# A graph-attention kernel's start-up: where the bound check's sums of squares, the last bias's rows and the residual additions stand

## The chip, the cores and the metric

The kernel runs on one core of a Trainium2 chip. The metric is device time in microseconds (us) of one execution, as a median of several runs. A core has five engines that work side by side, each through its own instructions in order: TensorE (PE in the profile, with PEld for its weight loads) multiplies matrices, VectorE (DVE) and ScalarE (ACT) do elementwise work and are the ones that read PE's results out of PSUM, GpSimd (POOL) does elementwise work in SBUF, and SyncE (SP) issues the DMA transfers. An instruction waits on semaphores until what it needs is there; everything behind it on the same engine waits with it.

## The reference

The input x is 64 graphs of 256 nodes with 512 features, in float32; all graphs share one adjacency matrix. Two layers follow, each on a layer norm with a ReLU, each added to x:

```python
h = jnp.maximum(_layernorm(x, axis=-1), 0.0)
x = x + _L0_gnn_ref(h, adj, L0_gnn_W, L0_gnn_a)
h = jnp.maximum(_layernorm(x, axis=-1), 0.0)
x = x + _L1_gnn_ref(h, adj, Wq, bq, Wk, bk, Wv, bv, Wo, bo)
```

The first is a graph attention: h W gives 256 features, their scores with two vectors are added pairwise, go through a leaky ReLU, a mask and a softmax, and weigh the same features; the result and h W stand side by side. The second is attention with 8 heads of 64 under the same mask, with the four weights Wq, Wk, Wv, Wo (512 x 512) and their biases.

## The kernel before

The 64 graphs are taken in 32 groups of two (GB = 2, NG = 32). Within a group, b is the graph and t one of its two tiles of 128 nodes. Everything stays in float32. Products with the weights are done in Strassen's manner with seven products instead of eight; for that the kernel adds and subtracts quarters of the weights once (`weight_sums`, `first_weight_sums`) and quarters of the operands in each group (`operand_sums`).

The softmax is done without subtracting the row's maximum. That is allowed only if the scores are bounded, so a bound check is computed from the weights: `judge` finds sums of squares of the weights and biases and some Gram matrices, and `conclude` turns these norms into a flag, `wrong`. If the flag is set, the whole work is done again by a general version (`any_inputs`); with the given inputs it is not.

Work is written as generators. Each `yield` ends a piece, and the main body calls `next` on them in an order written out by hand:

- `norms` is the first layer's norm over all groups (`first_norm`): mean and variance on VectorE (`measure`), the factor on GpSimd, xn on ScalarE, then a transposition of 32 x 32 blocks on VectorE into a tile xt, of which there is one buffer, written to DRAM (passed) and fetched back (moved) by DMA, and copied on ScalarE into hT0.
- `pieces` is the first layer for one group (`first_layer`): products ph, attention values e, products po, and the norm of the second layer through the same transposition into hT1.
- `products` is the second layer's projection of one group (`project`): for each of q, k and v seven products, in the order 1, 2, 6, 7, 5, 4, 3 of `seven`. Products 1, 6, 5 and 3 build up in one PSUM bank, 2, 4 and 7 in others. ScalarE copies intermediate sums out (kept_q, kept_k, kept_v; buffers with the tag "kept", three in turn), VectorE adds them to the later ones. PE may only go on with a bank when the copy or the addition that reads it is done.
- `verdict` is the bound check, and `bias` is `last_bias`: bv Wo + bo, added to the residual later. It makes the tile bv_rows on VectorE by four instructions from Wo and bv, sums it over the partitions by a matmul with a matrix of ones (pb), and adds bo to it (b_out).
- `residual(g)` adds b_out to x on GpSimd, two instructions for each graph.

In the start-up, group 0 goes through its first layer. Then the list `order` (line 1115) runs over the other 19 pieces of project(0); beside each stands which pieces of `norms` (n) and of `pieces` (s) follow. In this loop also stand the steps of the bound check (line 1127), of the last bias (line 1128), the weight sums of v and o and the residual addition for group 0 (line 1131).

Then comes the steady state: for each group g and each graph b in it, a string in `steps` (line 1135) orders the pieces. S computes the attention scores and exps of (g, b), m masks a pair of heads, u is a piece of project(g + 1), s one of first_layer(g + 2), n one of the norm of group g + 3, o one of the output products of the graph before (py, added into x by VectorE), f one of the row sums, r one of the residual and v a difference of values. weigh (products pr, then oT on VectorE) starts each graph.

`not_sooner` keeps an instruction behind the last one given to its engine in this way; other instructions may be moved a little by the scheduler of the framework. All matmuls keep the written order (`matmul`, line 136). Line 35 stands for all instructions of VectorE, ScalarE, GpSimd and most DMAs, and line 137 for all matmuls, since helpers record them; the names of tiles tell them apart.

Tiles with the same tag share buffers. In the version before, square_ones (the matrix of ones) lies in the buffer of o_sums, bv_rows in one of the three "kept" buffers, and squares, the output that nobody reads of the sums of squares, in the buffer of oT1.

Of the kernel before, what the change touches and what calls it, by code (L numbers as in the profile page):

```python
# [8 lines left out]
F32 = mybir.dt.float32  # L9
I32 = mybir.dt.int32  # L10
AF = mybir.ActivationFunctionType
ALU = mybir.AluOpType
AX = mybir.AxisListType

P = 128
# [8 lines left out]
LARGEST_VALUE = 1e4  # L24
# [33 lines left out]
def bounded(  # L58
# [27 lines left out]
    B, N, D = x.shape  # L86
    F1 = w0.shape[1]
    DH = 64
    HP = D // P
# [160 lines left out]
    gpsimd.memset(rexp, -0.5)  # L250
    ones = const.tile([P, S], F32, name="ones")
    gpsimd.memset(ones, 1.0)
    square_ones = big.tile([P, P], F32, tag="o_sums", name="square_ones", bufs=1)
    gpsimd.memset(square_ones, 1.0)

    def weight_sums(name, engine=vector):
# [16 lines left out]
    def last_bias():  # L273


        rows = att.tile([P, 2, D // 2], F32, tag="kept", name="bv_rows", bufs=3)
        for q in range(NQ):
            for half in range(2):
                of, by = w_sb["o"][:, half, 2 * q : 2 * q + 2, :], bv_col[:, half, q : q + 1]
                if q == half == 0:  # L280
                    not_sooner(vector, "tensor_scalar", rows, of, by, None, op0=ALU.mult)
                else:
                    vector.scalar_tensor_tensor(rows, of, by, rows, op0=ALU.mult, op1=ALU.add)
        yield
        pb = mm("pb")
        matmul(pb, square_ones, rows.rearrange("p o n -> p (o n)"), start=True, stop=True)
        yield
        not_sooner(vector, "tensor_add", b_out, pb, b_out)
        yield


    def judge():

        part = const.tile([P, 10], F32, name="part")
        vector.memset(part, 0.0)
        room = att.tile([P, 2 * HP + 1, P], F32, tag="p", name="room", bufs=1)
        heads = room[:, 2 * HP, :]  # L300
        vector.memset(heads, 0.0)
        for j in range(2):
            vector.memset(heads[j * DH : (j + 1) * DH, j * DH : (j + 1) * DH], 1.0)
        power = {}

        def bank(name):
            return mm(name).rearrange("p (h o) -> p h o", h=HP)

        for n, name in enumerate(("q", "k")):
            gram = bank(f"gram_{name}")  # L310
            for hp in range(HP):
                half, cols = hp // 2, slice(hp % 2 * P, (hp % 2 + 1) * P)
                for c in range(HP):
                    w = w_sb[name][:, c % 2, c // 2 * 2 + half, cols]
                    matmul(gram[:, hp, :], w, w, start=(c == 0), stop=(c == HP - 1))
            power[name] = room[:, n * HP : (n + 1) * HP, :]
            vector.tensor_mul(
                power[name], gram, heads[:, None, :].to_broadcast([P, HP, P])
            )
            yield  # L320
        for i in range(2):
            for n, name in enumerate(("q", "k")):
                square = bank(f"square_{name}{i}")
                for hp in range(HP):
                    a = power[name][:, hp, :]
                    matmul(square[:, hp, :], a, a, start=True, stop=True)
                if i < 1:
                    not_sooner(scalar, "copy", power[name], square)
                else:
                    scalar.activation(  # L330
                        power[name], square, AF.Square, accum_out=part[:, 8 + n : 9 + n]
                    )
                yield

        for _ in range(4):
            yield
        room = big.tile([P, D], F32, tag="oT1", name="squares", bufs=1)

        def squares(col, *srcs):
            sums = small.tile([P, HP], F32, tag="sums", name=f"sums{col}", bufs=2)  # L340
            for i, src in enumerate(srcs):
                to = room[:, : src.free_size()]
                if len(src.shape) == 3:
                    to = to.rearrange("p (a b) -> p a b", a=src.shape[1])
                not_sooner(
                    scalar, "activation", to, src, AF.Square, accum_out=sums[:, i : i + 1]
                )
            vector.reduce_sum(part[:, col : col + 1], sums[:, : len(srcs)], axis=AX.X)

        squares(2, *[w0_sb[:, c, 2:] for c in range(HP)])  # L350
        yield
        squares(3, *[w_sb["v"][:, :, i, :] for i in range(HP)])
        yield
        for i in range(2):
            squares(i, w0_sb[:, :, i])
        squares(4, bcol["q"])
        squares(5, bcol["k"])
        squares(6, bv_col)
        vector.reduce_max(part[:, 7:8], bad.rearrange("p a t -> p (a t)"), axis=AX.X)
        yield  # L360
        yield
        total = mm("total")[:, :10]
        matmul(total, square_ones, part, start=True, stop=True)
        norm = const.tile([P, 10], F32, name="norm")
        vector.tensor_scalar(norm, total, 1e-30, None, op0=ALU.add)
        power = const.tile([P, 10], F32, name="power")
        gpsimd.memset(power, 0.5)
        gpsimd.memset(power[:, 7:8], 1.0)
        gpsimd.memset(power[:, 8:10], 1.0 / 16)
        gpsimd.tensor_tensor(norm, norm, power, op=ALU.pow)  # L370
        norms_found.append(norm)
        yield
# [3 lines left out]
    def conclude():  # L376
        (norm,) = norms_found
        root = float(D) ** 0.5

        test = const.tile([P, 5], F32, name="test")  # L380
        side = const.tile([P, 2], F32, name="side")
        not_sooner(vector, "tensor_add", test[:, 0:1], norm[:, 0:1], norm[:, 1:2])
        vector.tensor_scalar(
            test[:, 0:1], test[:, 0:1], root / LARGEST_SCORE, None, op0=ALU.mult
        )
        not_sooner(vector, "tensor_scalar", side, norm[:, 8:10], root, None, op0=ALU.mult)
        vector.tensor_add(side, side, norm[:, 4:6])
        vector.tensor_mul(test[:, 1:2], side[:, 0:1], side[:, 1:2])
        vector.tensor_scalar(
            test[:, 1:2], test[:, 1:2], scale / LARGEST_SCORE, None, op0=ALU.mult  # L390
        )
        not_sooner(
            vector, "tensor_scalar",
            test[:, 2:3], norm[:, 2:3], root / LARGEST_VALUE, None, op0=ALU.mult
        )
        not_sooner(
            vector, "scalar_tensor_tensor",
            test[:, 3:4], norm[:, 3:4], root, norm[:, 6:7], op0=ALU.mult, op1=ALU.add
        )
        vector.tensor_scalar(  # L400
            test[:, 3:4], test[:, 3:4], 1.0 / LARGEST_VALUE, None, op0=ALU.mult
        )
        not_sooner(vector, "tensor_scalar", test[:, 4:5], norm[:, 7:8], 2.0, None, op0=ALU.mult)
        vector.tensor_scalar(test, test, 1.0, None, op0=ALU.is_le)
        held = const.tile([P, 1], F32, name="held")
        vector.tensor_reduce(held, test, axis=AX.X, op=ALU.min)
        vector.tensor_scalar(wrong, held[0:1, :], -1.0, 1.0, op0=ALU.mult, op1=ALU.add)
# [660 lines left out]
    def run(part):  # L1068
        for _ in part:
            pass  # L1070
# [40 lines left out]
    next(pieces)  # L1111
    next(verdict)
    next(verdict)
    next(norms)
    order = "n - s n sn - - ss ss s s - - - - s - s -".split()
    for i, parts in enumerate(order, 2):
        next(products)
        if i == 14:
            weight_sums("o", gpsimd)
        if i == 9:  # L1120
            first_weight_sums()
        if i in (2, 8):
            weight_sums("kv"[i // 7])
        for part in parts:
            if part != "-":
                next(norms if part == "n" else pieces, None)
        next(verdict, None)
        if i in (12, 14, 15):
            next(bias)
        if i == 17:  # L1130
            run(residual(0))
    run(verdict)


    steps = ("Smmnfuuuumonmnuofuusssosfsfssuvnofunonfosuo", "Ssmmfusmusmfuososfuosfrsuuonufrounfouunsous")
# [1 line left out]
    for g in range(NG):  # L1137
        products = project(g + 1) if g + 1 < NG else iter(())
        pieces = first_layer(g + 2) if g + 2 < NG else iter(())
        for b, parts in enumerate(steps):  # L1140
            if g == b == 0:

                parts = "Smmnfuuumnmnuufuussssfsfssuvnfunnfsuu"
            elif g == NG - 1:
                parts = "Smmoomoomooo"
            if waiting is not None:
                weigh(*waiting)
                late = outputs(*waiting[:2])
            i, count = -1, sum(part not in "frv" for part in parts)
            additions = residual(g + 1) if b == 1 and g + 1 < NG else iter(())  # L1150
            for part in parts:
                i += part not in "frv"
                if part == "u":
# [25 lines left out]
                if i == count // 2:  # L1179
                    if g == max(NG - 2, 0) and b == 1:  # L1180
                        conclude()
                    if g + 3 < NG:
                        load(g + 3, b)
        run(products)
        run(pieces)
    run(late)
# [372 lines left out]
```

## Time and profile before

| | us |
|---|---|
| median of 3 runs (2410.87 to 2412.3) | 2410.94 |
| the profiled execution, its own time | 2410.2 |
| its span, first to last instruction | 2408.5 |
| PE busy | 2380.4 (99%) |
| VectorE busy | 1687.9 (70%) |
| GpSimd busy | 1417.0 (59%) |
| ScalarE busy | 1022.0 (42%) |
| mean granted PE clock, as a share of full speed | 0.998 |
| PE busy from 0 to 20 / 20 to 40 / 40 to 60 us | 10.5 / 19.9 / 18.1 |
| PE busy from 60 to 80 / 80 to 100 / 100 to 120 us | 17.7 / 12.8 / 19.7 |
| PE clock from 60 to 80 / 80 to 100 us | 0.91 / 0.83 |

The span is one execution as the profiler recorded it; a little lies around it, so its own time is longer. Line by line, the timeline gives the start, the duration, the engine, the operation, the tile written and the tiles read, their shapes, and in brackets how long the engine was idle before and what ended that. A list of waits adds these idle times by pairs. Idle time of an engine that nobody waits for costs nothing.

### The profile page before, as it was taken

The page shows a single profiled execution, that of the slowest core. Times are in us where ns is not written, and L with a number is a line of the kernel's source. Part 1 is how long each engine was busy: PE and PEld are TensorE (multiplying, and loading weights), DVE is VectorE, ACT ScalarE, POOL GpSimd, SP SyncE. Part 2 cuts the span into 40 slices and gives each one's busy share as a digit, 9 for nine tenths or more (in the row PEclk, how much of TensorE's full clock was granted, in tenths as well). Part 3 has the DMA queues.
Part 4 walks back from the last instruction along what each step waited for, and adds up shares of the span by engine and source line. Part 5 has one row for each costly group of instructions (what it writes and reads, how often), then busy time and mean ns, then how long its engine had stood idle before and what let it go on. Part 6 is the DMA issues. An engine that isn't in the chain of part 4 may idle for free.

```text
span 2408.5 us, 42960 instructions
## 1 busy us (share of the span) xinstructions
PE 2380.4 (99%) x15772; PEld 2005.6 (83%) x15772; DVE 1687.9 (70%) x3338; ACT 1022.0 (42%) x2017; POOL 1417.0 (59%) x1282
## 2 busy tenths in 40 slices
PE   8899999999999999999999999999999999999998
PEld 7688888888888888888888888888888888888886
DVE  7576766777667767667777677776677676676665
ACT  5444443444444444434444444444344444343431
POOL 3566657555566556565556665565655565655652
PEclk9999999999999999999999999999999999999999
DMA  6244455544454444555444544444454445444331
GB/s 210 75 141 139 138 158 148 154 151 136 140 161 150 145 145 136 154 151 160 149 138 138 157 148 154 141 143 143 153 167 145 136 136 159 150 148 152 110 106 46
DMA packets 272041, 343.76 MB, mean 143 GB/s; under 512 B 25424, under 2 KB 217168, under 8 KB 271824
## 3 DMA queue, kind: packets, MB, share of 16 engines
q1 hardware_dynamic: 271824, 340.95, 45.8%
q8 instruction: 126, 2.06, 0.4%
q14 instruction: 91, 0.75, 0.1%
HBM read 177.22 MB, written 163.64 MB: 142 GB/s over the span
## 4 chain that ended last, share of the span: by engine, by line
PE 96%; DVE 1%; DMA 1%; ACT 1%; issue 0%; POOL 0%; SPq 0%; DVEq 0%; ACTq 0%; POOLq 0%
PE pv L137 16%; PE py L137 16%; PE pq L137 16%; PE pk L137 16%; PE sc L137 10%; PE pr L137 9%; PE ph L137 8%; PE po L137 4%; DMA w_sb<-in_L_gnn_W_dram 0%; DVE st L35 0%; DVE bv_rows L35 0%; DVE x L35 0%; ACT xn L35 0%; PE total L137 0%; DMA own<-line 0%
## 5 line engine op out<-in xcount | busy, mean ns | idle before, releaser
L35 POOL TENSOR_TENSOR p<-p 128x512 f32<-128x512 f32 x248 | 380.7, 1547 | 492.2 <-DVE p L35 478.7
L35 ACT ACTIVATE xn<-x,factor 128x512 f32<-128x512 f32 x256 | 194.4, 806 | 322.3 <-POOL factor L35 322.2
L35 DVE TENSOR_TENSOR p<-p,maskT 128x1024 f32<-128x1024 f32 x254 | 325.8, 1302 | 3.7 <-ACT p L35 3.7
L35 DVE TENSOR_TENSOR x<-py,x 128x256 f32<-128x256 f32 x448 | 186.0, 416 | 192.0 <-PE py L137 185.8
L35 ACT ACTIVATE p<-sc 128x512 f32<-128x512 f32 x512 | 257.6, 625 | 145.0 <-PE sc L137 128.3
L35 POOL TENSOR_TENSOR parts<-parts 128x512 f32<-128x512 f32 x248 | 248.5, 1002 | 82.6 <-DMA parts<-rows 59.0
L137 PE MATMUL py<-wo_sb,oT 128*128 128x256 f32 x1024 | 262.4, 379 | 0.6 <-DVE oT L35 0.6
L137 PE MATMUL sc<-q,k 64*128 64x256 f32 x2048 | 252.4, 390 | 0.6 <-DVE oT L35 0.6
L137 PEld LDWEIGHTS sc<-q,k 64*128 64x128 f32 x2048 | 204.5, 186 | 49.0 <-issue 25.9
L137 PE MATMUL pk<-hT,wk_sb 128*128 128x256 f32 x1024 | 244.7, 382 | 0.0
L137 PE MATMUL pq<-hT,wq_sb 128*128 128x256 f32 x1024 | 240.0, 382 | 0.3 <-ACT kept_q L35 0.3
L137 PE MATMUL pv<-wv_sb,hT 128*128 128x256 f32 x1024 | 238.4, 381 | 1.0 <-DVE k L35 1.0
L137 PE MATMUL pr<-p,v 128*32 128x256 f32 x4096 | 234.2, 380 | 0.0
L137 PEld LDWEIGHTS pq<-hT,wq_sb 128*128 128x128 f32 x1024 | 191.8, 190 | 35.8 <-issue 9.9
L35 POOL TENSOR_TENSOR factor<-factor,rexp 128x2 f32<-128x2 f32 x128 | 120.8, 943 | 169.0 <-DVE factor L35 168.8
L137 PEld LDWEIGHTS pv<-wv_sb,hT 128*128 128x128 f32 x1024 | 195.6, 191 | 29.2 <-DVE k L35 1.4
L137 PEld LDWEIGHTS py<-wo_sb,oT 128*128 128x128 f32 x1024 | 194.2, 190 | 28.2 <-DVE oT L35 1.1
L137 PEld LDWEIGHTS pk<-hT,wk_sb 128*128 128x128 f32 x1024 | 189.7, 190 | 33.3 <-issue 9.9
L137 PEld LDWEIGHTS pr<-p,v 128*32 128x32 f32 x4096 | 126.8, 110 | 97.8 <-issue 15.6
L137 PE MATMUL py<-wo_sb,o_sums 128*128 128x256 f32 x768 | 197.6, 380 | 0.5 <-DVE x L35 0.5
L137 PE MATMUL pk<-sums,wk_sb 128*128 128x256 f32 x768 | 182.8, 381 | 2.3 <-ACT kept_k L35 2.3
L137 PE MATMUL pq<-sums,wq_sb 128*128 128x256 f32 x768 | 181.5, 379 | 1.9 <-ACT kept_q L35 1.9
(148 smaller groups left out, 4055.7 us busy)
## 6 DMA issues: line engine op xcount, KB each, us to landing
passed<-xt SPq DMA_DIRECT2D x124, 512.0 KB, 3.1
moved<-passed SPq DMA_DIRECT2D x496, 128.0 KB, 3.4
rows<-p SPq DMA_DIRECT2D x124, 512.0 KB, 3.4
parts<-rows SPq DMA_DIRECT2D x496, 128.0 KB, 3.0
x<-in_x_dram SPq DMA_DIRECT2D x64, 512.0 KB, 4.4
out_dram<-x SPq DMA_DIRECT2D x62, 512.0 KB, 4.0
own<-line SPq DMA_DIRECT2D x31, 256.0 KB, 3.1
wq_sb<-in_L_gnn_Wq_dram SPq DMA_DIRECT2D x2, 512.0 KB, 9.2
```

Of the source, the lines that this page charges most:

```text
L35: instruction = getattr(self.engine, operation)(*args, **kwargs)
L137: in_order(nc.tensor.matmul(*args, **kwargs))
```

## The change

Five edits belong together.

1. The sums of squares leave the start-up. The loop over `order` no longer steps the bound check; instead each group from g = 2 on steps it once, in its second graph (at the ninth counted piece), until it is through: the first layer's weight in group 2, Wv in group 3, the score columns in group 4, the biases in group 5, the matmul `total` and the roots in group 6. The squares' unread output takes a "kept" buffer each time, since oT1 is in use by then. By that time the weights hold the sums and differences for the seven products, so the norms of two of them are multiplied by the square root of 3 (`changed`), a looser bound. The first layer's weight is taken with its two score columns (258 instead of 256 numbers).
2. square_ones gets a buffer of its own.
3. bv_rows lies in the buffer of oT0. Its first piece stands where it stood, after piece 12 of project(0); the matmul pb comes after piece 18 instead of 14 and the addition to b_out after piece 19 instead of 15.
4. In `order`, pieces of the norm of group 2 move: they came at pieces 1 (ahead of the list), 2, 5 and 6 and now come at 3, 5, 13 and 15. The weight sums of v move from piece 8 to 7, those of the first layer from 9 to 5, those of o from 14 to 13.
5. The residual additions of all groups form one sequence, of which each r takes the next piece. Those of group 0 leave the start-up: the string of the first graph gets an r, and the last graph of all gets one too. In each group, the two places take (g, 1) and (g + 1, 0) instead of (g + 1, 0) and (g + 1, 1).

```diff
@@ -250,7 +250,7 @@
     gpsimd.memset(rexp, -0.5)
     ones = const.tile([P, S], F32, name="ones")
     gpsimd.memset(ones, 1.0)
-    square_ones = big.tile([P, P], F32, tag="o_sums", name="square_ones", bufs=1)
+    square_ones = const.tile([P, P], F32, name="square_ones")
     gpsimd.memset(square_ones, 1.0)
 
     def weight_sums(name, engine=vector):
@@ -273,7 +273,7 @@
     def last_bias():
 
 
-        rows = att.tile([P, 2, D // 2], F32, tag="kept", name="bv_rows", bufs=3)
+        rows = big.tile([P, 2, D // 2], F32, tag="oT0", name="bv_rows", bufs=1)
         for q in range(NQ):
             for half in range(2):
                 of, by = w_sb["o"][:, half, 2 * q : 2 * q + 2, :], bv_col[:, half, q : q + 1]
@@ -332,12 +332,9 @@
                     )
                 yield
 
-        for _ in range(4):
-            yield
-        room = big.tile([P, D], F32, tag="oT1", name="squares", bufs=1)
-
         def squares(col, *srcs):
             sums = small.tile([P, HP], F32, tag="sums", name=f"sums{col}", bufs=2)
+            room = att.tile([P, D], F32, tag="kept", name=f"squares{col}", bufs=3)
             for i, src in enumerate(srcs):
                 to = room[:, : src.free_size()]
                 if len(src.shape) == 3:
@@ -347,17 +344,17 @@
                 )
             vector.reduce_sum(part[:, col : col + 1], sums[:, : len(srcs)], axis=AX.X)
 
-        squares(2, *[w0_sb[:, c, 2:] for c in range(HP)])
+        squares(2, *[w0_sb[:, c, :] for c in range(HP)])
         yield
         squares(3, *[w_sb["v"][:, :, i, :] for i in range(HP)])
         yield
         for i in range(2):
             squares(i, w0_sb[:, :, i])
+        yield
         squares(4, bcol["q"])
         squares(5, bcol["k"])
         squares(6, bv_col)
         vector.reduce_max(part[:, 7:8], bad.rearrange("p a t -> p (a t)"), axis=AX.X)
-        yield
         yield
         total = mm("total")[:, :10]
         matmul(total, square_ones, part, start=True, stop=True)
@@ -376,6 +373,9 @@
     def conclude():
         (norm,) = norms_found
         root = float(D) ** 0.5
+
+
+        changed = 3.0**0.5
 
         test = const.tile([P, 5], F32, name="test")
         side = const.tile([P, 2], F32, name="side")
@@ -391,11 +391,11 @@
         )
         not_sooner(
             vector, "tensor_scalar",
-            test[:, 2:3], norm[:, 2:3], root / LARGEST_VALUE, None, op0=ALU.mult
+            test[:, 2:3], norm[:, 2:3], changed * root / LARGEST_VALUE, None, op0=ALU.mult
         )
         not_sooner(
             vector, "scalar_tensor_tensor",
-            test[:, 3:4], norm[:, 3:4], root, norm[:, 6:7], op0=ALU.mult, op1=ALU.add
+            test[:, 3:4], norm[:, 3:4], changed * root, norm[:, 6:7], op0=ALU.mult, op1=ALU.add
         )
         vector.tensor_scalar(
             test[:, 3:4], test[:, 3:4], 1.0 / LARGEST_VALUE, None, op0=ALU.mult
@@ -1111,25 +1111,21 @@
     next(pieces)
     next(verdict)
     next(verdict)
-    next(norms)
-    order = "n - s n sn - - ss ss s s - - - - s - s -".split()
+    order = "- n s n s - - ss ss s s n - n - s - s -".split()
     for i, parts in enumerate(order, 2):
         next(products)
-        if i == 14:
+        if i == 13:
             weight_sums("o", gpsimd)
-        if i == 9:
+        if i == 5:
             first_weight_sums()
-        if i in (2, 8):
+        if i in (2, 7):
             weight_sums("kv"[i // 7])
         for part in parts:
             if part != "-":
                 next(norms if part == "n" else pieces, None)
-        next(verdict, None)
-        if i in (12, 14, 15):
+        if i in (12, 18, 19):
             next(bias)
-        if i == 17:
-            run(residual(0))
-    run(verdict)
+    additions = (piece for g in range(NG) for piece in residual(g))
 
 
     steps = ("Smmnfuuuumonmnuofuusssosfsfssuvnofunonfosuo", "Ssmmfusmusmfuososfuosfrsuuonufrounfouunsous")
@@ -1140,14 +1136,13 @@
         for b, parts in enumerate(steps):
             if g == b == 0:
 
-                parts = "Smmnfuuumnmnuufuussssfsfssuvnfunnfsuu"
+                parts = "Smmnfuuumnmnuufuussssfsfssuvnfrunnfsuu"
             elif g == NG - 1:
-                parts = "Smmoomoomooo"
+                parts = ("Smmoomoomooo", "Smrmoomoomooo")[b]
             if waiting is not None:
                 weigh(*waiting)
                 late = outputs(*waiting[:2])
             i, count = -1, sum(part not in "frv" for part in parts)
-            additions = residual(g + 1) if b == 1 and g + 1 < NG else iter(())
             for part in parts:
                 i += part not in "frv"
                 if part == "u":
@@ -1181,6 +1176,8 @@
                         conclude()
                     if g + 3 < NG:
                         load(g + 3, b)
+                if b == 1 and i == 8 and g >= 2:
+                    next(verdict, None)
         run(products)
         run(pieces)
     run(late)
```

## The prediction

> **What bounds the kernel now.** I read the page first. TensorE is busy for nearly the whole span:
>
> ```profile
> PE 2380.4 (99%) x15772; PEld 2005.6 (83%) x15772; DVE 1687.9 (70%) x3338; ACT 1022.0 (42%) x2017; POOL 1417.0 (59%) x1282
> ```
>
> So only 28.1 us of idle TensorE (2408.5 - 2380.4), and time at a reduced clock, can be won. The list of TensorE's waits says where they are (us in total, times, longest):
>
> ```profile
> PE pb L137 <- DVE bv_rows L35: 6.2, 1, 6.2
> PE pk L137 <- ACT kept_k L35: 2.3, 1, 2.3
> PE pq L137 <- ACT kept_q L35: 2.2, 2, 1.9
> ...
> PE pv L137 <- DVE k L35: 1.0, 1, 1.0
> ```
>
> Each happens once, in the start-up. From 140 to 2370 us the table by stretches shows PE busy for all of every stretch I asked for (200.00 of 200.00 from 200 to 400). TensorE's timeline places the waits (start, us, in brackets idle before):
>
> ```profile
> 65.73 3.16 PE L137 MATMUL pk<-sums,wk_sb 128*128 128x256 f32 x8 [2.34 <-ACT kept_k L35]
> 68.69 2.46 PE L137 MATMUL po<-H,e 128*128 128x257 f32 x8
> ...
> 81.00 1.99 PE L137 MATMUL pv<-wv_sb,hT 128*128 128x256 f32 x8 [0.99 <-DVE k L35]
> 89.19 2.08 PE L137 MATMUL pb<-bv_rows,square_ones 128*128 128x512 f32 x2 [6.19 <-DVE bv_rows L35]
> 91.05 3.21 PE L137 MATMUL pv<-wv_sb,hT 128*128 128x256 f32 x8
> ```
>
> Eight matmuls of 256 columns normally start 1.73 us apart. After the two long waits they take 2.96 (65.73 to 68.69) and 3.05: the granted clock is 0.60 and 0.55 from 66 to 70, and 0.50 to 0.57 from 88 to 94. Each long wait is paid for again. The timeline of all engines shows who is late:
>
> ```profile
> 62.84 0.41 ACT L35 ACTIVATE squares<-w_sb 128x256 f32<-128x256 f32 x1
> ...
> 64.86 0.82 ACT L35 ACTIVATE kept_k<-pk,bk_sb 128x256 f32<-128x256 f32 x2
> ...
> 83.12 1.30 DVE L35 STREAM_TRANSPOSE xt<-xn 128x512 f32<-128x512 f32 x2 [2.17 <-DMA passed<-xt]
> 84.34 0.45 DVE L35 TENSOR_SCALAR bv_rows<-wo_sb,bv_col 128x512 f32<-128x512 f32 x1
> 84.83 4.31 DVE L35 SCALAR_TENSOR_TENSOR bv_rows<-wo_sb,bv_col,bv_rows 128x512 f32<-128x512 f32 x3
> ```
>
> kept_k stands behind four squares on ScalarE; bv_rows stands on VectorE behind a transpose that waits for its only xt buffer to be written out.
>
> **The Trainium skill.** "TensorE: Matmul & The Clock Gate", Part 1 (the HAM clock gate): the clock halves after an idle window of about 3.4 us and is restored after about as long of work, in free-running windows. The trace agrees: about 4 us near half clock after 2.34 and after 6.19 us, none after 1.89. "SBUF — State Buffer", Who interferes with whom: VectorE with two SBUF inputs and GpSimd exclude each other. The trace agrees: o_sums takes 0.42 us alone, 1.38 to 1.49 beside GpSimd (320.3 to 324.4). "DMA: Bandwidth & Descriptors", the SWDGE path's anatomy, gives about 2.0 us fixed; these transfers go by SP, so I use the trace: xt freed 2.6 us after issue.
>
> **The change on the path.** From pq at 50.72 to the first sc at 102.82 are 52.1 us. Work in it: 18 products at 1.73, two po pairs at 1.73, pb 0.86 (512 columns), total 0.14, and 0.33 of issue: 35.9. The other 16.2 are waits (1.89 + 2.34 + 0.99 + 6.19 = 11.4), reduced clock (5.25 for pk and po against 3.45, 4.91 for pb and pv against 2.58: 4.1) and restarts (0.7). I replay this stretch in the new order with the old durations.
>
> kept_q: xn of group 2 (GpSimd's factor is there at 52.2) now stands behind both kept_q, not ahead. They run at 50.9 and 52.6; pq goes on at 52.44 instead of 54.49, saving 2.05. The next two pq follow without a wait, and pk starts at 57.6.
>
> kept_k: xn of group 2's second half and 4 squares leave ScalarE. It does e (own still lands at 56.3), exp to 60.2, q to 60.95, kept_k to 61.7; pk waits 0.7 from 61.05 instead of 2.34. That is shorter than the 1.89 that cost no clock, so 1.8 comes back too. pk runs at 61.75 instead of 65.73, its end 5.2 earlier; total's 0.14 leaves; last pk ends at 73.85.
>
> pv and bv_rows: factor at 72.1, xt transposes to 73.4, k to 74.05; pv at 74.1 (wait 0.25), 6.9 early. The next transposes still wait for xt (73.4 + 2.6 = 76.05), end 77.4; bv_rows follows: 0.45, a v addition, then 0.75 + 1.86 + 1.64 beside GpSimd's wo_sb, done at 82.85. But pb now stands behind five pv products, ending at 82.7: wait 0.15 for 6.19, no clock loss (2.3). After pb and two pv, sc starts at 87.6: **15.2 us earlier**. Bounds for this step: 16.3 if nothing remains, 11 if half the replayed margins fail and the clock dips once.
>
> **What the moves may cost.** The second xt of group 2 is moved past two kept_v, two v additions and, on SP, past passed and moved of group 1 (1 + 4 + 1 + 4 issues, 1.74 us per four). Replayed: transposes end at 87.7, passed lands at 90.4; moved waits as before for its buffer (ScalarE's hT copies), lands near 97. Those hT copies also slip behind four exps, ending at 91.7 (4.1 us after sc starts, before 1.7), so GpSimd's sums begin 2.3 us later against TensorE; its pair additions then overlap less with VectorE, and about 0.5 of the lag is left where ph needs group 2's sums. Before, they were 0.4 to 0.7 ahead. Cost 0.3, between -0.3 and 1.5 (oT to sc then had 0.56 of wait already).
>
> b_out leaves the way of sc's banks: added at 88.4, the fifth bank is needed at 89.5. Four residual additions (4.95 us) leave GpSimd at 95.7; two go into its 10.1 us idle at 133, two into the later slots. In each group the two slots keep their number of additions and take x one half later: ready at 305.7, needed by output additions some 20 us later. Without that cover, up to 2.5 us a group.
>
> Squares in the steady steps stand on ScalarE after the third kept_k:
>
> ```profile
> 289.18 0.84 ACT L35 ACTIVATE kept_k<-pk,bk_sb 128x256 f32<-128x256 f32 x2 [0.69 <-PE pk L137]
> 297.85 1.52 ACT L35 ACTIVATE xn<-x,factor 128x512 f32<-128x512 f32 x2 [7.82 <-POOL factor L35]
> ```
>
> Four of w0 take 4 x 0.54 = 2.2 us, four of wv 4 x 0.75 = 3.0, the small ones 0.33 each; all fit in 7.82. Without cover: 2.2 + 3.0 + 0.7 + 1.0 = 6.9. What waits behind them on ScalarE is that xn, then k and pv's copies; VectorE waits for them in eight reductions of 0.16 that stand after po's second reciprocal (293.3), when the squares are over (293.0 at the latest). Their buffer, one of three of the kept kind, was last read by the k addition of the same project, long done. In group 6, total is 0.14 on TensorE, and GpSimd's power (1.96 us) now stands ahead of a pair sum and of factor; behind them are xn, moved and the row sums, with 0.5 to 2 us of slack. I take 0.2 in all (0 to 1). square_ones' own buffer and three multiplications by a constant cost nothing: no instruction more.
>
> The end: the last half's two residual additions now follow GpSimd's mask there, in the last stretch:
>
> ```profile
> 2367.40 2.43 POOL L35 TENSOR_TENSOR p<-p,maskT 128x1024 f32<-128x1024 f32 x1 [9.80 <-ACT p L35]
> ...
> 2370.32 1.22 DVE L35 TENSOR_TENSOR p<-p,maskT 128x1024 f32<-128x1024 f32 x1
> ```
>
> They run from 2369.8 to 2372.4 beside two such VectorE masks, which take 1.7 to 2.25 beside GpSimd elsewhere (181.25, 111.57). py's additions wait behind the masks, and TensorE behind these (0.26 and 0.20 idle already). Cost 1.2, between 0 and 2.
>
> Sum: 15.2 - 0.3 - 0.2 - 1.2 = **13.5 us**. The profiled execution took 2410.2 (span 2408.5 and 1.7 around it): 2396.7. It lies 0.7 below the median 2410.94, so **2397.4**.
>
> **Rivals.**
> (A) As summed: 2395.5 to 2399.5, chance 0.62.
> (B) Part of the start-up wait comes back: bv_rows later than the five pv products, or group 1's sums later. For it: margins of 0.15 and 0.5 us. Against: all precede with the same durations. A 2.3 us wait with its 1.8 of clock, or both ends of the costs above: gain 7 to 11, 2399.5 to 2404; 0.23.
> (C) The spread squares are not hidden, and stall TensorE in five groups: 13.5 - 6.9, about 2404 to 2408. The 7.82 us speaks against: 0.07.
> (D) Slower: the residual additions, now half a group later, make py's additions wait in about 30 groups. Decides from 13.5 / 30 = 0.45 us a group; with 1 us, 2427. Against: 20 us of margin; and from the ninth group on nothing but the half of x in these additions differs in the order of any engine: 0.04.
> (E) It does not do what it says: the check with the looser sqrt(3) bound fails and the whole work is done again, above 4000 us. A W of 512 x 256 at variance 1/512 has norm 16; 16 x 1.73 x 22.6 / 10000 = 0.06, far from 1: under 0.01. Better than A (no contention at the end): 0.03.
>
> **The numbers.** Time: A's 2397.4. The range takes A, what is better, and B: 2393 to 2404.5. A difference of 0.2%, 4.8 us, is about what a measurement of this kernel can tell. Faster: better and A and B but for a little, and some of C: 0.90; same: rest of B and C: 0.06; slower: D, E: 0.04.
>
> **What would show it.** TensorE's waits: pb under 1 us, pk by kept_k near 0.7, none of 1.9 by kept_q; clock 1.00 from 60 to 100; first sc of group 0 near 87.6; PE still full from 140 to 2365; masks near the end above 1.5 us. Wrong would be: a new wait of ph or pq on GpSimd's sums near 95 to 110, of pb on bv_rows above 2 us, or idle TensorE in groups 2 to 6.

## The result, and the profile after

The changed kernel takes 2400.05 us (median of 5 runs, 2398.31 to 2401.28); the kernel before, in runs beside it, 2410.94 (2410.36 to 2413.55). The ratio is 0.9952, with a 95% interval of 0.9937 to 0.9967: 11 us or 0.5% faster, 2.6 us less than the 13.5 predicted. Run a second time, beside the first experiments, it took 2398.18 (2397.80 to 2398.51) against 2411.88, 13.7 us faster. One kernel thus moves by 2 to 3 us from one session to the next.

The page's line of TensorE (PE) keeps its 99% in a shorter span:

```profile
PE 2378.2 (99%) x15772; PEld 2005.0 (84%) x15772; DVE 1693.1 (71%) x3338; ACT 1021.4 (43%) x2017; POOL 1418.4 (59%) x1282
```

TensorE's list of waits (us in total, times, longest) has lost pb's wait of 6.2 and the kept_q wait of 1.9; in their place stands one for oT, and a small one for GpSimd's sums:

```profile
PE sc L137 <- DVE oT L35: 2.0, 1, 2.0
PE ph L137 <- DVE prod L35: 1.9, 1, 1.9
PE py L137 <- DVE x L35: 1.3, 3, 0.9
...
PE ph L137 <- POOL sums_xn L35: 0.5, 1, 0.5
PE pk L137 <- ACT kept_k L35: 0.5, 1, 0.5
```

TensorE's timeline of the changed kernel shows the start-up without a gap from pv to the first scores, pb taking its 0.86 us between two products, and then the two new waits:

```profile
63.05 1.99 PE L137 MATMUL pk<-sums,wk_sb 128*128 128x256 f32 x8 [0.52 <-ACT kept_k L35]
...
75.27 3.72 PE L137 MATMUL pv<-wv_sb,hT 128*128 128x256 f32 x16
...
84.00 1.02 PE L137 MATMUL pb<-bv_rows,square_ones 128*128 128x512 f32 x2
...
88.41 3.92 PE L137 MATMUL sc<-q,k 64*128 64x256 f32 x32
...
107.55 1.16 PE L137 MATMUL ph<-w_more,sums_xn 128*128 128x129 f32 x8 [0.55 <-POOL sums_xn L35]
...
126.63 4.40 PE L137 MATMUL sc<-q,k 64*128 64x256 f32 x22 [2.00 <-DVE oT L35]
```

ScalarE makes kept_k right after q, and VectorE has bv_rows ready at 82.9 (79.70 + 3.21), 1.1 us before TensorE asks for it:

```profile
61.44 0.82 ACT L35 ACTIVATE q<-pq,bq_sb 128x256 f32<-128x256 f32 x2
62.15 0.84 ACT L35 ACTIVATE kept_k<-pk,bk_sb 128x256 f32<-128x256 f32 x2
...
78.60 0.45 DVE L35 TENSOR_SCALAR bv_rows<-wo_sb,bv_col 128x512 f32<-128x512 f32 x1
79.09 0.69 DVE L35 TENSOR_TENSOR v<-pv,kept_v 128x512 f32<-128x512 f32 x1
79.70 3.21 DVE L35 SCALAR_TENSOR_TENSOR bv_rows<-wo_sb,bv_col,bv_rows 128x512 f32<-128x512 f32 x3
```

The squares now stand on ScalarE in the steady steps (here group 2), and the xn behind them still waits for its factor:

```profile
278.01 0.84 ACT L35 ACTIVATE kept_k<-pk,bk_sb 128x256 f32<-128x256 f32 x2 [0.69 <-PE pk L137]
278.74 0.42 ACT L35 ACTIVATE squares<-w_sb 128x258 f32<-128x258 f32 x1
...
280.68 0.19 ACT L35 ACTIVATION_READ_ACCUMULATOR squares<-w_sb 128x1 f32 x1
287.35 1.52 ACT L35 ACTIVATE xn<-x,factor 128x512 f32<-128x512 f32 x2 [6.48 <-POOL factor L35]
```

In the last group, the residual on GpSimd runs beside two of VectorE's masks, and py waits behind them:

```profile
2359.30 3.48 POOL L35 TENSOR_TENSOR x<-x,b_out 128x512 f32<-128x512 f32 x2
2359.83 1.82 DVE L35 TENSOR_TENSOR p<-p,maskT 128x1024 f32<-128x1024 f32 x1
...
2362.04 1.13 PE L137 MATMUL py<-wo_sb,o_sums 128*128 128x256 f32 x4 [0.86 <-DVE x L35]
2362.24 1.62 DVE L35 TENSOR_TENSOR p<-p,maskT 128x1024 f32<-128x1024 f32 x1
```

Cutting the span at marks that every kernel has shows where the time went. The marks are TensorE's first product pq on sums, its first pv, its first sc, the pk product after the second score stage, and the pr products of the last graph; each number is a difference of two starts in the timelines.

| stretch, us | before | after | after again |
|---|---|---|---|
| start to pq | 48.99 | 50.27 | 50.44 |
| pq to pv | 32.01 | 25.00 | 24.58 |
| pv to sc | 21.82 | 13.14 | 13.14 |
| sc to pk | 39.32 | 42.55 | 40.16 |
| pk to the last pr | 2250.44 | 2252.16 | 2252.12 |
| last pr to end | 15.92 | 16.38 | 16.16 |
| span | 2408.5 | 2399.5 | 2396.6 |

The start-up gave 15.7 and 16.1 us between pq and sc. Of it, 3.2 in the first trace but only 0.8 in the second went back between sc and pk, 1.7 between pk and the last pr, and 0.2 to 0.5 after it; 1.3 to 1.5 were lost before the first pq.

### The profile page after: what moved, and what is told of

Its sections match the earlier page's. It is cut to its first block, busy times and chain, and to the rows that moved or that the text cites. A ratio compares the mean times of both kernels' runs of the same rounds, so it can differ in the third digit from the quotient of the medians.

```text
span 2399.5 us, 42951 instructions
## 1 busy us (share of the span) xinstructions
PE 2378.2 (99%) x15772; PEld 2005.0 (84%) x15772; DVE 1693.1 (71%) x3338; ACT 1021.4 (43%) x2017; POOL 1418.4 (59%) x1282
## 4 chain that ended last, share of the span: by engine, by line
PE 96%; DMA 1%; DVE 1%; ACT 1%; POOL 0%; issue 0%; SPq 0%; ACTq 0%; DVEq 0%; POOLq 0%
PE pv L137 16%; PE pk L137 16%; PE py L137 16%; PE pq L137 16%; PE sc L137 10%; PE pr L137 9%; PE ph L137 8%; PE po L137 4%; DMA x<-in_x_dram 0%; SPq L35 0%; DMA w_sb<-in_L_gnn_W_dram 0%; ACT e L35 0%; DMA line<-rows 0%; POOL x L35 0%; POOL parts L35 0%
## 5 line engine op out<-in xcount | busy, mean ns | idle before, releaser
L35 POOL TENSOR_TENSOR factor<-factor,rexp 128x2 f32<-128x2 f32 x128 | 115.6, 903 | 179.9 <-DVE factor L35 179.7
```

Of the source, the lines that this page charges most:

```text
L35: instruction = getattr(self.engine, operation)(*args, **kwargs)
```

## The experiments

The first four runs are of one session, on one chip, beside the kernel before at 2411.88 us; the last four are of a later one, on another chip, beside the kernel before at 2410.76. Where a run of the second session is compared with the repeat, which is of the first, a difference of 2 to 3 us in the time alone proves little, and the stretches of the traces decide.

**The changed kernel again.** No edit. It is there to tell what the change does from what varies by itself.

> The changed kernel a second time, unaltered, as the measure of what varies from one profiled execution to the next. Two things of its first trace are not explained by any instruction that the change moves: TensorE was already 1.28 us late at the first product of the projection (pq at 50.27 us, before 48.99), and the DMA that brings own for group 2 took 4.7 us from issue to landing (before 3.7), which made TensorE wait 2.00 us for oT ahead of the second score stage and cost 1.1 us of clock. If both vary by chance, this trace shows pq near 49 and own landing in 3 to 3.8 us, the wait for oT near 1.0 (0.56 of before and some 0.5 for the later sums of group 1), and a span near 2397. Rival: the residual additions, which now run on GpSimd just then (120.17 to 122.69), delay own or the e behind it; then the wait of 2.0 us and the 1.1 us of clock come back here, whatever the start does.

Measured: 2398.18 us against 2411.88 beside it, ratio 0.9942 (0.9929 to 0.9956). The late start stayed (50.44), the wait for oT fell to 0.71 us with no loss of clock. The two traces' lists of DMA issues in the window around it (KB each, us from issue to landing) show why, first that of the first trace, then that of the repeat:

```profile
own<-line SPq DMA_DIRECT2D x1, 256.0 KB, 4.7
```

```profile
own<-line SPq DMA_DIRECT2D x1, 256.0 KB, 3.4
```

The residual stands at the same place in both, so the rival falls: what made 2.00 us of 0.71 is own's landing. In the first trace e's wait was put down to the residual (3.00 <-POOL x); but own landed 0.1 us before e there, and in the repeat e starts while the residual is still running:

```profile
119.94 2.54 POOL L35 TENSOR_TENSOR x<-x,b_out 128x512 f32<-128x512 f32 x2
121.20 1.71 ACT L35 ACTIVATE e<-own,H 128x256 f32<-128x256 f32 x4 [1.71 <-DMA own<-line]
```

So e doesn't wait for the residual, and the label named the wrong partner of a wait that has several. All five traces with the changed order on ScalarE (below) bear it out: own landed after 4.7, 4.2, 3.7, 3.4 and 3.0 us, and sc waited 2.00, 1.52, 1.03, 0.71 and 0.66. Why own's landing varies was not tested.

The start to pq is not explained by any edit; it lies between 48.25 and 50.44 in the traces. Of the 1.28 us between the first two traces, 0.63 is the landing of the first weight (VectorE's prod began at 10.43 us before, 11.06 after), and the rest is the first group of 16 products ph, which took 5.69 us before, 6.34 after and 6.79 in the repeat. What sets these is open.

**Bias and residual alone.** Edits 2, 3 and 5 on the kernel before:

```diff
-        if i in (12, 14, 15):
+        if i in (12, 18, 19):
             next(bias)
-        if i == 17:
-            run(residual(0))
     run(verdict)
+    additions = (piece for g in range(NG) for piece in residual(g))
```

with the two buffers and the strings as in the change.

> The kernel before with edits 2, 3 and 5 only: last bias's rows in the buffer of oT0 and pb four pieces later, and the residual additions in one sequence; the squares and the norm pieces stay where they were. From the timeline of before: pv starts at 81.0 as before, four more products follow without a wait, bv_rows is ready at 89.1 and pb comes at 89.65. My theory, that each edit's own wait goes and the gains add: pb's wait of 6.19 falls below 0.5, its 2.3 us of reduced clock goes, the first sc comes 8.5 to 8.8 us earlier against pq; the end costs 1.1 and the group-0 residual 0 to 1, so 2403.5 (7 us faster). Rival, that the norm pieces and squares carry the gain: pb still waits several us for bv_rows and this kernel is within 2 us of before.

Measured: 2404.68 us (2403.52 to 2405.66), ratio 0.9970 (0.9957 to 0.9982), 7.2 us faster; pb waits for nothing. TensorE's timeline:

```profile
66.84 2.00 PE L137 MATMUL pk<-sums,wk_sb 128*128 128x256 f32 x8 [2.34 <-ACT kept_k L35]
68.68 1.90 PE L137 MATMUL po<-H,e 128*128 128x257 f32 x8
...
79.09 1.99 PE L137 MATMUL pk<-sums,wk_sb 128*128 128x256 f32 x8 [1.37 <-DVE k L35]
82.12 3.72 PE L137 MATMUL pv<-wv_sb,hT 128*128 128x256 f32 x16 [1.04 <-DVE k L35]
...
90.93 1.13 PE L137 MATMUL pb<-bv_rows,square_ones 128*128 128x512 f32 x2
```

From pq to pv it takes 32.01 us, as before to the hundredth; from pv to sc 13.32 instead of 21.82. Two things follow. The bias edit is worth 8.5 us, all of it after pv. (No run has edit 3 without edit 5, but between pv and sc TensorE waited for nothing but bv_rows before, so the residual had no part in it.) And the reduced clock after pk's wait was worth nothing by itself here: the same wait of 2.34 us cost no clock this time (1.84 us from pk to po instead of 2.96), but the time came back as a wait of 1.37 for k on VectorE. VectorE's chain, with the reductions of the squares in it, was later than TensorE. These are its first reciprocals of po, before and here:

```profile
70.81 0.16 DVE L35 RECIPROCAL ri<-po 128x1 f32<-128x1 f32 x1
71.92 0.16 DVE L35 RECIPROCAL ri<-po 128x1 f32<-128x1 f32 x1
```

Counted from pq, they start at 21.82 and 21.81 us, though po itself came 1.1 us sooner here (18.57 for 19.70).

Two waits of the changed kernel are in this kernel too, with the norm pieces in the old order. So they don't come from edit 4:

```profile
114.59 1.16 PE L137 MATMUL ph<-w_more,sums_xn 128*128 128x129 f32 x8 [0.55 <-POOL sums_xn L35]
...
132.32 3.29 PE L137 MATMUL sc<-q,k 64*128 64x256 f32 x22 [0.66 <-DVE oT L35]
```

**Squares alone.** Edits 1 and 2 on the kernel before (the squares take the form of the change, `order` and the rest that of before):

```diff
-        next(verdict, None)
         if i in (12, 14, 15):
             next(bias)
@@
+                if b == 1 and i == 8 and g >= 2:
+                    next(verdict, None)
```

> The kernel before with edits 1 and 2 only: squares spread over the steady steps. My theory: four squares (2.0 us with their reads) leave the way of kept_k, pk waits 0.3 instead of 2.34 us and its 1.2 to 1.8 us of reduced clock goes; all that follows is 3.8 us earlier, since the chain through po, the factor, the two transposes and bv_rows is paced by it, and pb still waits 6.2 us. Steady steps cost 0.6. In all 3.2 us faster, 2407.7. Rival 1: pb's wait absorbs it, since bv_rows is ready no sooner: within 1 us of before. Rival 2: the squares are not hidden in groups 2 to 6, up to 6.9 us are lost again: slower than before by 3.

Measured: 2405.05 us (2404.81 to 2406.55), ratio 0.9974 (0.9964 to 0.9984), 6.8 us faster, twice what I expected. pq to pv takes 27.40 us (4.6 less): pk's wait 2.02, clock 1.79, total 0.14, and some 0.7 of waiting for k ahead of pv, which I had not counted. pv to sc takes 1.4 less, 1.07 of it in pb's wait, since bv_rows' three instructions took 3.21 us here and 4.31 before. In both, GpSimd's additions for wo_sb run beside them. Which of the two engines is held up differs, first before, then here:

```profile
85.61 1.85 DVE L35 SCALAR_TENSOR_TENSOR bv_rows<-wo_sb,bv_col,bv_rows 128x512 f32<-128x512 f32 x1
85.66 1.26 POOL L35 TENSOR_TENSOR wo_sb<-wo_sb 128x512 f32<-128x512 f32 x1 [5.51 <-DVE bv_rows L35]
...
81.45 0.75 DVE L35 SCALAR_TENSOR_TENSOR bv_rows<-wo_sb,bv_col,bv_rows 128x512 f32<-128x512 f32 x1
81.56 1.76 POOL L35 TENSOR_TENSOR wo_sb<-wo_sb 128x512 f32<-128x512 f32 x1 [4.19 <-DVE bv_rows L35]
```

pb still waits, and still costs clock:

```profile
83.93 2.08 PE L137 MATMUL pb<-bv_rows,square_ones 128*128 128x512 f32 x2 [5.12 <-DVE bv_rows L35]
85.80 2.87 PE L137 MATMUL pv<-wv_sb,hT 128*128 128x256 f32 x8
88.50 1.89 PE L137 MATMUL pv<-wv_sb,sums 128*128 128x256 f32 x8
```

The stretch from pk to the last pr is 0.54 us longer than before. Neither rival holds.

**Squares and norm pieces.** Edits 1, 2 and 4, with the bias at pieces 12, 14 and 15, its buffer and the residual as before (the diff is against the changed kernel, and leaves out the buffer and the strings):

```diff
-        if i in (12, 18, 19):
+        if i in (12, 14, 15):
             next(bias)
-    additions = (piece for g in range(NG) for piece in residual(g))
+        if i == 17:
+            run(residual(0))
```

> The kernel before with edits 1, 2 and 4: squares spread and the norm pieces and weight sums reordered, the last bias and the residual as before. My theory: kept_q's 1.9 us and kept_k's 2.34 us and its clock go, pv starts 6.9 us earlier; bv_rows stands behind the second transposition, which waits for its xt buffer as before, so pb still waits 6 to 6.5 us and costs 2.3 us of clock: the first sc comes 7 us earlier against pq. With 0.5 to 1 for group 1's later sums and the steady squares this is 6 us faster, 2405. With the 7 of the bias and residual alone it would make up the whole gain of 11 to 13.5, so the edits add. Rival, that pb's wait takes over what is saved ahead of it: less than 2 us faster, the wait for bv_rows then near 11 us.

Measured: 2403.25 us (2401.89 to 2404.93), ratio 0.9964 (0.9951 to 0.9978), 8.6 us faster (6 expected). pq to pv takes 24.58 us, exactly as in the repeat of the changed kernel, 7.4 less than before; pv to sc 21.74, as before, with pb waiting 5.43 and then 3.0 us of clock lost:

```profile
80.52 2.08 PE L137 MATMUL pb<-bv_rows,square_ones 128*128 128x512 f32 x2 [5.43 <-DVE bv_rows L35]
```

So the gain splits cleanly: edits 1 and 4 make pq to pv, edit 3 makes pv to sc, and from pq to sc the two sum up (7.5 + 8.5 = 16.0, with all edits 16.1). The ScalarE order of before is kept here, and ph and sc wait for nothing, with edit 4 in.

**Without the norm pieces.** The changed kernel with `order`, the weight sums' places and the first norm piece of before:

```diff
+    next(norms)
-    order = "- n s n s - - ss ss s s n - n - s - s -".split()
+    order = "n - s n sn - - ss ss s s - - - - s - s -".split()
```

> The changed kernel without edit 4: squares spread, last bias and residual moved, but the norm pieces and weight sums in the order of before. The runs so far gave, from the first product on sums (pq) to the first score product, 8.5 us for the bias and residual alone, 6.0 for the squares alone and 7.5 for squares with norms. If the edits add, the first score product comes 14.5 us earlier here (39.3 us after pq, before 53.83), with the wait of 1.9 us for kept_q back, and the kernel is about 1.5 us slower than the changed one: 2399.7. Rival, that pb's wait hid the norm pieces' gain and without it edit 4 is worth more: kept_q's 1.9 and a wait of pv or sc for k come back, 3 us or more slower than the changed kernel, 2401.5.

Measured: 2400.71 us (2399.25 to 2402.11), ratio 0.9959 (0.9946 to 0.9973), 2.5 us slower than the repeat. pq to sc takes 40.53 us, not 39.3: edit 4 is worth 2.8 us here and 1.5 without edit 3. My theory, that the edits add, missed this; the rival's 3 us is nearer, and for its reason: without edit 3, pb's wait and its clock swallowed 1.3 us of what edit 4 saves. kept_q's wait is back:

```profile
53.75 1.99 PE L137 MATMUL pq<-sums,wq_sb 128*128 128x256 f32 x8 [1.88 <-ACT kept_q L35]
```

**An order on ScalarE.** The changed kernel, with one condition taken out in `scores`:

```diff
-                    others = [last, *put_last] if i > 1 else [last]
+                    others = [last, *put_last]
```

In the changed kernel the framework's scheduler set four exps ahead of the last copies into hT of group 1. The bias and residual kernel has that order too, the kernels without edits 3 and 5 have that of before; which of these two edits brings it, no run shows. ScalarE's timeline of the repeat:

```profile
88.27 0.58 ACT L35 COPY v<-pv 128x512 f32<-128x512 f32 x1 [0.59 <-PE pv L137]
89.33 2.06 ACT L35 ACTIVATE p<-sc 128x512 f32<-128x512 f32 x4 [0.47 <-PE sc L137]
91.25 1.16 ACT L35 COPY hT<-moved 128x512 f32<-128x512 f32 x2
```

> The changed kernel with one order fixed: on ScalarE the last two copies into hT of group 1 stand ahead of the first four exps of group 0, as they did before, by listing them among what each exp must follow. My theory now: the 0.55 us that ph waits for the sums of group 2 and the 0.7 us that sc then waits for oT come from these copies standing behind four exps (GpSimd's sums begin 4.3 us after the first score product, before 1.8), which came with edits 3 and 5 and not with the moved norm pieces. Then both waits go, the stretch from the first score product to the product after the second scores falls from 40.2 us to 38.8, and the kernel is 1.3 us faster than the changed one: 2396.9. Rival: the waits come from the residual additions in the way of GpSimd's sums; then nothing changes.

Measured: 2395.37 us (2394.74 to 2397.08), ratio 0.9937 (0.9923 to 0.9950), 2.8 us faster than the repeat, and 2.5 faster than the kernel with the squares twice, which ran beside it. ScalarE's and GpSimd's timelines:

```profile
87.09 0.58 ACT L35 COPY v<-pv 128x512 f32<-128x512 f32 x1 [0.59 <-PE pv L137]
87.58 1.14 ACT L35 COPY hT<-moved 128x512 f32<-128x512 f32 x2
88.62 4.01 ACT L35 ACTIVATE p<-sc 128x512 f32<-128x512 f32 x8
...
88.79 1.26 POOL L35 TENSOR_TENSOR sums<-hT 128x512 f32<-128x512 f32 x1 [4.84 <-ACT hT L35]
```

GpSimd's sums begin 1.8 us after the first sc (86.99) instead of 4.3; ph and sc wait for nothing, and sc to pk takes 38.82 us, 1.34 less than in the repeat. The other 1.2 of its shorter span is its start to pq, 49.27. The residual additions stand where they stood, so the rival falls. That sc waits for nothing needs own to land early as well: it took 3.2 us here. The kernel before has the same order, and with own landing after 3.7 us its sc waited 0.56.

**And the last residual sooner.** The same, and:

```diff
+            elif g == NG - 2 and b == 1:
+                parts = parts.replace("frounf", "frrounf")
             elif g == NG - 1:
-                parts = ("Smmoomoomooo", "Smrmoomoomooo")[b]
+                parts = "Smmoomoomooo"
```

> The same order fixed on ScalarE, and the last residual piece, for the second graph of the last group, moved from that graph's own stage to the stage before (group 30, second graph, beside the residual of group 31). My theory: the 1.0 us that the last but one stage lost in all kernels with edit 5 is the residual addition on GpSimd holding up VectorE's masks (1.82 and 1.62 us instead of 1.22); with it gone the stretch from the last but one pr to the last falls back to 16.1 us. Together with the 1.3 above 2.3 us faster than the changed kernel: 2395.9. Rival: those additions only move their price into the stage of group 30: then 2396.9.

Measured: 2394.32 us (2394.03 to 2395.77), ratio 0.9932 (0.9919 to 0.9946): 16.4 us faster than before, and the fastest of all. GpSimd's residual now runs before the last group, and VectorE's masks there are short again:

```profile
2340.43 4.95 POOL L35 TENSOR_TENSOR x<-x,b_out 128x512 f32<-128x512 f32 x4
...
2354.68 1.22 DVE L35 TENSOR_TENSOR p<-p,maskT 128x1024 f32<-128x1024 f32 x1
```

The stage of the last group's first graph, from the start of its pr to the next one, took 17.1 us in every kernel with edit 5 as it is, and 16.1 before and here; the stages of group 30 did not grow. Span 2392.9 against 2394.1 of the kernel with the ScalarE order alone; the time differs by 1.05.

**Squares twice.** The changed kernel with each large square made two times:

```diff
-                not_sooner(
-                    scalar, "activation", to, src, AF.Square, accum_out=sums[:, i : i + 1]
-                )
+                for _ in range(2 if col in (2, 3) else 1):
+                    not_sooner(
+                        scalar, "activation", to, src, AF.Square, accum_out=sums[:, i : i + 1]
+                    )
```

> The changed kernel with each square of the first layer's weight (group 2) and of Wv (group 3) made twice: 2.4 us and 3.2 us more on ScalarE in these two groups, and the same results. Theory: they stand in ScalarE's idle time (6.5 and 5.6 us are left there until xn), so the stages of groups 2 and 3 keep their length within 0.1 us and the time is that of the changed kernel, 2398.2, within 1 us. Rival C, squares are not hidden: these stages grow by up to 5.6 us, 2401 to 2404.

Measured: 2397.83 us (2396.77 to 2398.66), ratio 0.9945 (0.9932 to 0.9959), the repeat's time. ScalarE in group 3, at the last square of Wv:

```profile
354.81 0.19 ACT L35 ACTIVATION_READ_ACCUMULATOR squares<-wv_sb 128x1 f32 x1
356.40 1.52 ACT L35 ACTIVATE xn<-x,factor 128x512 f32<-128x512 f32 x2 [1.41 <-POOL factor L35]
```

Even with double the work 1.41 us of idle time are left, and the stages of groups 2 and 3 with squares in them keep their length within 0.03 us. Rival C falls.

## Why the prediction was right or wrong

Faster was right, and so was the mechanism of most of it, rival A's. The first measurement, 2400.05 us for 2397.4, is inside the range, but in the stretch that the prediction gave to rival B (2399.5 to 2404), and half of B came true: group 1's sums were later, and ph waited for them at 107.55, one of the signs named there as wrong. B's other half, late bv_rows, did not. The repeat, 2398.18, lies in A's stretch. That its 13.7 us come so near 13.5 is in part luck: its trace is only 11.9 us shorter than that of before, and the rest is that the kernel before ran 1.7 us slower in that session than in its trace. By its steps:

- **kept_q and kept_k** were right. kept_q's long wait went; pk waited 0.52 us (0.7 expected), and in the repeat not at all. pq to pv came out 7.0 and 7.4 us shorter for 6.9. The term of 1.8 for the clock ("each long wait is paid for again"), though, was not a price of its own: the bias and residual kernel lost no clock after the same wait and reached pv no sooner. With edit 1, which also takes the reductions out of VectorE's way, it was won.
- **pv and bv_rows** were right: pb waited for nothing (0.15 expected), and pv to sc fell by 8.7 us for 8.3. Without edits 1 and 4, 8.5 were won. The margin of 1.1 us was luck: bv_rows' last three instructions took 3.21 us, where the replay had 4.25, because in the kernels with edit 1 GpSimd and not VectorE was held up, which the replay did not have. With 4.32, in the bias and residual kernel, they ended 0.05 us before pb.
- **What the moves may cost** is the step that failed, in size and cause. Expected 0.3 us, at most 1.5; measured 3.2 in the profiled execution, 0.8 in the repeat. That the hT copies would slip behind four exps and make GpSimd's sums late was foreseen, and ph waited the 0.55 that "about 0.5 of the lag" meant. I put it down to the second xt of group 2, which edit 4 moves; the bias and residual kernel has it with the old norm order, and the squares and norm pieces kernel, with edit 4, does not. Setting the copies ahead of the exps again took it all away, in traces where own landed early. And the step stopped at ph: H is then late too, own is issued later, and sc waits 0.7 on top. The rest up to 2.00, and the 1.1 us of clock after it, is own's landing, 4.7 us here and 3.4 in the repeat, which I had taken as fixed.
- **The residual** of group 0, costed at nothing, cost nothing that a run shows. The second halves' move by half a group made no output addition late, so rival D falls: the stages from group 7 to group 30 of the changed kernel are those of before to 0.01 us each.
- **The squares**, taken at 0.2 us, cost 0.22, all in group 6, where `total` now is (0.14 of it left the start-up). Another 0.35 in one stage of the changed kernel (group 3, first graph) stands where no square is; in other kernels such an extra of 0.24 to 0.36 falls in other stages, or nowhere. What makes it is open.
- **The end**, 1.2 expected, was 1.0: masks of 1.82 and 1.62 us instead of 1.22, and py's waits of 0.86 and 0.22. (At 111.57 the trace of before has 2.28 us for a mask beside GpSimd, where the prediction read 2.25.) The last stretch had another 0.2 to 0.5, not explained.
- The late start of 1.3 us in the first trace was in no step, and belongs to none of the edits as far as the runs show.

So against the sum of 13.5, start-up +0.5, group 1 and own -2.9, the late start -1.3, and smaller terms make the 8.9 us between the two profiled executions (2410.2 and 2401.28); the repeat, with own landing in 3.4 us, took 2398.35.

## What to carry to other kernels

Where a wait ahead of a long one is removed, price everything up to the next instruction that several chains meet in, not the wait itself: here the reduced clock at pk was covered by VectorE's lateness, and only the edit that took work from both ScalarE and VectorE won it. After an edit, look also at the order of instructions that it doesn't name: the scheduler set copies into hT behind four exps, and GpSimd and TensorE came late behind them. One line that fixes their order took 1.3 us from the stretch of sc to pk, about what edit 4 is worth without edit 3 (1.5). And when a wait has several partners, don't trust its label: look for a trace in which the named partner is still running when the wait ends.

## What the runs showed of the hardware

- How long a wait is does not alone decide whether TensorE's clock drops. After waits of 1.52 and 1.89 us none was lost, after 2.00 us 1.1 (the granted clock was 0.59 and 0.55 from 126 to 130 us), after the same wait of 2.34 us 1.8 in one kernel and nothing in another, after 5.12, 5.43 and 6.19 us 2.0, 3.0 and 2.3. The Trainium skill ("TensorE: Matmul & The Clock Gate", Part 1) puts the idle window after which the clock halves at about 3.4 us and lets the windows run freely. Free windows would allow the same 2.34 us to cost something once and nothing another time, which was not tested. That waits of 2.00 and 2.34 us, shorter than that window, cost clock at all differs from the page (the prediction called it agreement), and here the measurement decides.
- A small broadcast through DRAM (own, 256 KB in SBUF from one line of 2 KB) took 4.7 and 3.4 us to land at the same place in two executions of the same kernel, and 3.0 to 4.2 there in its variants.
- Two residual additions beside VectorE's masks took 3.48 us instead of 2.5, and the masks 1.82 and 1.62 instead of 1.22. This agrees with the Trainium skill ("SBUF — State Buffer", Who interferes with whom), by which a VectorE instruction with two inputs in SBUF contends with a GpSimd instruction that reads SBUF.
- Which of the two pays can turn on a few hundredths of a microsecond. Where GpSimd's addition for wo_sb started 0.04 to 0.05 us after bv_rows (before, and in the bias and residual kernel), VectorE took 1.85 us instead of 0.75; where it started 0.10 to 0.11 us after (the other eight traces), VectorE took 0.75 and GpSimd 1.76 instead of 1.26. That the head start decides is read from these starts, not tested by itself.
